# Two factors taken out of the build order's reckoning in a Mamba and mixture-of-experts layer

## The chip, the cores and the metric

The kernel runs on one core of one Trainium2 chip. The metric is the device time of one execution in microseconds (us). Engines: PE is TensorE (matmuls and transposes; its weight loads are listed apart as PEld), DVE is VectorE, ACT is ScalarE, POOL is GpSimd, SP is SyncE, which here only issues DMAs.

## The reference

One layer on x of 4 sequences x 1024 steps x 512 channels, all float32. Cut to what matters:

```python
sa, ca, ga, sb, cb, gb = modulation(silu(c) @ wmod)      # per sequence, 6 x 512
h = layernorm(x) * (1 + ca) + sa
u = causal_depthwise_conv(h, conv_w, 4 taps) + conv_b
dt, Bm, Cm = split(u @ xproj_w.T, [128, 16, 16])
delta = softplus(dt @ dtproj_w.T + dtproj_b)
# scan over time, 16 states for each of 512 channels
h_t = exp(delta * A) * h_(t-1) + delta * u * Bm ;  y_t = sum_n h_t[n] * Cm[n]
x = x + ga * (y + u * D_skip)
h = layernorm(x) * (1 + cb) + sb
logits = tanh(h @ Wg1.T) @ Wg2.T                         # 8 experts, the top 2 chosen
down[e] = silu(h @ Wup[e].T + bup[e]) @ Wdown[e].T + bdown[e]     # 512 -> 256 -> 512
x = x + gb * sum_e scores[e] * down[e]
```

## The kernel before

**Blocks and stages.** Time is cut into blocks of 512 steps: two for each of the first three sequences, and 512, 384 and 128 for the last, eight blocks in all. `front(blk)` makes the layernorm, convolution and projections of a block. The recurrence takes a block as 128 units, one for each of 16 states and 4 chunks of 128 channels. For a unit the steps are:

- `products_b` (L892 on ACT, or L899 on POOL): dB, the product of delta * u with a column of B, with time on partitions, in buffers of two units;
- `inputs` (L935, PE): up to four transposes of dB into the PSUM tile pb, of which there are two;
- `decays` (L920, ACT): exp(delta * A) into the tile h, four buffers of two units;
- `recurrences` (L950, DVE): the scan along time, from h and pb, in place in h;
- `products_c` (L967, POOL): hc = h * C, C's row having come by a broadcast load cq (L868, issued on SP, four buffers); then a copy of the last state (L975);
- `sums` (L1006, PE): transposes of hc that accumulate over the 16 states in PSUM.

`back(blk)` then makes the second layernorm and the router and scatters each token's row, for its two experts, to a DRAM buffer sorted by expert (L1335, an indirect DMA of POOL). `tiles(g)` and `expert` take 128 sorted rows at a time, 86 tiles in all: a load of the rows and of the expert's weights (1,025 KB, issued on SP, four buffers `w`), transposes (L1407), the first product (L1420), bias, tanh and gate (L1431, L1438, L1440), the second product (L1448), the scaling (L1458) and a store. `combine` fetches the rows back by indirect DMAs that add (L1497). The last block of 128 tokens goes instead through all eight experts (`dense`, L1550 to L1615).

**The order.** Nothing is scheduled on the chip: each engine runs its instructions in the order in which the builder wrote them. The builder writes them by a reckoning of its own, the class `Order`. Each piece of work above is a generator, a thread, that yields one step at a time: an engine (or a choice of engines), a cost, and what it depends on. `run` finds the step that could start first, looks at the steps on the same engine that could start within `TOGETHER` (0.15 us) after that, and takes the one whose thread has the earliest due time. It moves the engine's clock on by the cost, says when the result may be used (`HANDOFF`: 0.30 us after PE, 0.17 after DVE, 0.22 after ACT, 0.12 after POOL), and lets the generator go on, which writes the instructions. Buffers are handed out in the same reckoned time, so the order sets which buffer a tile gets too. Threads with a due time below `URGENT` (the last two blocks') get a window of 0.8 us (`AHEAD`).

The costs are formulas in the number n of elements per partition: a matmul `t_mm` 2 x 0.00084 n us (a float32 product is two instructions), a transpose `t_tr` 0.11, ACT `t_act` 0.19 + 0.00083 n, DVE `t_dve` 0.09 + 0.00104 n, a scan `t_scan` 0.09 + 0.00215 n, POOL `t_pool` 0.05 + 0.0024 n. Where a step leaves the engine open (`either`, `both`, `products_b`), `begins` chooses by these bare costs. A transfer is reckoned at 290 KB/us shared, 150 KB/us alone, and 4.0 us besides (L107). Due times go by 150 us for a block of 512 steps (`DUE`, L265).

Between the formula and the engine's clock stand two factors (L101, L102, used at L234 and L235): every cost over 0.03 us is multiplied by `PACE`, which is 1.1 for PE and 1.0 for the others, and `WAIT` is added, 0.06 us on DVE, ACT and POOL.

Of the kernel before, what the change touches and what calls it, by code (L numbers as in the profile page):

```python
# [97 lines left out]

PE, DVE, ACT, POOL, SP = range(5)
HANDOFF = (0.30, 0.17, 0.22, 0.12, 0.0)  # L100
PACE = (1.1, 1.0, 1.0, 1.0, 1.0)  # L101
WAIT = (0.0, 0.06, 0.06, 0.06, 0.0)  # L102
TOGETHER = 0.15
URGENT = -1e3
AHEAD = 0.8
# [78 lines left out]
class Order:  # L184
# [34 lines left out]
    def run(self):  # L219
        while self.threads:  # L220
            can = [(b, th) for th in self.threads if (b := self.begins(th)) is not None]
            if not can:
                raise RuntimeError("no thread can go on: " + str([th[0].__name__ for th in self.threads]))
            t0, eng, _ = min(can, key=lambda c: c[0][0])[0]
            (t, _, cost), th = min(
                (
                    c
                    for c in can
                    if c[0][1] == eng and c[0][0] <= t0 + (AHEAD if c[1][3] < URGENT else TOGETHER)
                ),  # L230
                key=lambda c: c[1][3],
            )
            self.eng, kb = eng, th[1][4]
            if cost > 0.03:  # L234
                cost = cost * PACE[eng] + WAIT[eng]  # L235
            self.start = t
            self.free[eng] = t + cost
            self.fin = t + cost + HANDOFF[eng]
            if kb:
                self.moved[eng] = max(self.moved[eng], t + cost) + kb / KB_PER_US  # L240
                self.fin = max(self.moved[eng], t + cost + kb / KB_ALONE) + TRANSFER
            th[2] = self.fin
            th[3] += th[4]
            self.advance(th)
# [1486 lines left out]
```

## Time and profile before

| | before |
|---|---|
| three runs | 1471.55, 1481.65, 1467.81 us; median 1471.55 |
| profiled execution | 1473.26 us; its span from first to last instruction 1471.5 us |
| mean granted TensorE clock | 0.925 of full speed |
| busy: PE, DVE, ACT, POOL | 1236.6, 1146.8, 1041.7, 1052.8 us |
| weight loads (PEld) | 931.7 us |
| DMA | 321.65 MB, mean 219 GB/s |
| first scan starts, last scan starts | 67.7 us, 1387.6 us |

Busy time is the time in which an engine executes; waits, semaphore instructions and the issuing of DMAs are not counted. The ends of matmuls are modelled, so PE's busy time is no measure of how near it is to its peak. The granted clock is the share of TensorE's full speed that the chip allowed in a stretch. A wait is shown as "engine, tile, line <- what ended it".

### The profile page before, as it was taken

The numbers are of one execution on the slowest core, as the hardware profiler recorded it, in microseconds if no ns is written. First come the engines' busy times: TensorE is split into PE (matmuls) and PEld (weight loads), VectorE is DVE, ScalarE is ACT, GpSimd is POOL, SyncE is SP. The second block draws the span as 40 slices with busy tenths as digits, with TensorE's granted clock in tenths as the row PEclk, the third lists the DMA queues.
The fourth block names the chain that finished last, engine by engine and source line by source line (L and its number), as shares of the span: only waits on it lengthen the run. The fifth ranks groups of instructions, "written<-read, shape, count | busy, mean of one in ns | idle before, by whom it ended". The sixth has DMA issues, their size and how long they took to land. (4 is left out here: it accounts for less than half of the span.)

```text
span 1471.5 us, 24433 instructions
## 1 busy us (share of the span) xinstructions
PE 1236.6 (84%) x7716; PEld 931.7 (63%) x7716; DVE 1146.8 (78%) x1860; ACT 1041.7 (71%) x2086; POOL 1052.8 (72%) x1239
## 2 busy tenths in 40 slices
PE   5588777878788988988888888998798898888886
PEld 1447564656477766775667766786587776764653
DVE  3569999889887898998887888897879879556343
ACT  3679898689687684899676776888678877455210
POOL 1368897898687676888888656798788878656222
PEclk8699899889799998999699999999999999998798
DMA  4367664758688997654679968688999986986997
GB/s 175 101 161 157 136 160 101 197 127 199 140 243 283 292 273 202 213 159 101 197 257 313 309 210 204 219 269 246 262 252 271 281 221 219 337 249 200 298 311 200
DMA packets 141935, 321.65 MB, mean 219 GB/s; under 512 B 14899, under 2 KB 43475, under 8 KB 128998
## 3 DMA queue, kind: packets, MB, share of 16 engines
q1 hardware_dynamic: 111344, 254.35, 57.9%
q0 software_dynamic: 13888, 32.58, 9.9%
q10 hardware_dynamic: 16566, 33.08, 8.8%
q8 instruction: 63, 1.03, 0.3%
q14 instruction: 74, 0.61, 0.1%
HBM read 245.95 MB, written 82.40 MB: 223 GB/s over the span
## 5 line engine op out<-in xcount | busy, mean ns | idle before, releaser
L967 POOL TENSOR_TENSOR hc<-h,cq 128x512 f32<-128x512 f32 (+2 forms) x576 | 689.5, 1255 | 190.1 <-PE acc L1006 53.4
L920 ACT ACTIVATE h<-delta,a_neg 128x512 f32<-128x512 f32 (+2 forms) x576 | 370.8, 667 | 88.8 <-POOL state L975 44.9
L892 ACT ACTIVATE dB<-duT,bT 128x256 f32<-128x256 f32 x801 | 359.9, 499 | 77.2 <-PE pb L935 74.8
L935 PE MATMUL pb<-ident,dB 128*128 128x128 f32 x2048 | 344.6, 291 | 80.4 <-DVE h L950 64.3
L1006 PE MATMUL acc<-ident,hc 128*128 128x128 f32 x2048 | 340.9, 291 | 75.1 <-POOL hc L967 73.2
L950 DVE TENSOR_TENSOR_SCAN h<-h,state,pb 128x512 f32<-128x512 f32 (+2 forms) x320 | 330.6, 1054 | 50.9 <-PE pb L935 25.8
L935 PEld LDWEIGHTS pb<-ident,dB 128*128 128x128 f32 x2048 | 251.2, 149 | 169.3 <-DVE h L950 85.9
L1006 PEld LDWEIGHTS acc<-ident,hc 128*128 128x128 f32 x2048 | 250.5, 148 | 155.9 <-POOL hc L967 122.3
L950 DVE TENSOR_TENSOR_SCAN h<-h,pb 128x512 f32<-128x512 f32 x256 | 304.4, 1207 | 45.9 <-PE pb L935 37.2
L1420 PE MATMUL pe<-xT,w 128*128 128x128 f32 x1376 | 188.0, 282 | 6.5 <-ACT xT L351 4.8
L1420 PEld LDWEIGHTS pe<-xT,w 128*128 128x128 f32 x1376 | 174.1, 197 | 27.4 <-issue 14.2
L1448 PE MATMUL po<-w,hid 128*128 128x512 f32 x344 | 180.8, 612 | 6.6 <-DVE hid L1440 6.5
L899 POOL TENSOR_TENSOR dB<-duT,bT 128x512 f32<-128x512 f32 (+1 forms) x115 | 119.6, 1061 | 18.4 <-PE pb L935 12.4
L1497 POOL DMA_INDIRECT xc<-xs,idx x56 | 90.4, 1614 | 51.7 <-DMA xc<-xs,idx 29.8
L1458 DVE SCALAR_TENSOR_TENSOR xs<-po,xs,gbh 128x512 f32<-128x512 f32 x86 | 63.6, 740 | 39.7 <-PE po L1448 38.1
L1335 POOL DMA_INDIRECT xs<-h,idx x62 | 64.0, 1032 | 41.3 <-POOL idx L1334 9.2
L1448 PEld LDWEIGHTS po<-w,hid 128*128 128x128 f32 x344 | 54.1, 195 | 24.0 <-issue 11.3
L1438 ACT ACTIVATE th<-pe 128x256 f32<-128x256 f32 x86 | 32.2, 377 | 49.4 <-DVE pe L1431 49.2
L351 ACT COPY xT<-px 128x512 f32<-128x512 f32 x79 | 45.5, 577 | 25.0 <-PE px L1407 24.5
L975 POOL COPY state<-h 128x2 f32<-128x2 f32 x160 | 54.6, 341 | 0.1
L720 PE MATMUL pxd<-xpg,u 128*128 128x160 f32 x256 | 46.2, 329 | 9.4 <-issue 5.6
L1407 PE MATMUL px<-ident,xs 128*128 128x128 f32 x344 | 53.8, 284 | 0.3 <-DVE u L688 0.3
(196 smaller groups left out, 1533.5 us busy)
## 6 DMA issues: line engine op xcount, KB each, us to landing
w<-w_all SPq DMA_DIRECT2D x86, 1025.0 KB, 8.5
cq<-scr SPq DMA_DIRECT2D x224, 256.0 KB, 5.3
xs<-xs SPq DMA_DIRECT2D x86, 256.5 KB, 5.3
xs<-xs SPq DMA_DIRECT2D x86, 256.0 KB, 8.0
xs<-xc ACTq DMA_DIRECT2D x16, 1026.0 KB, 11.7
we<-w_all SPq DMA_DIRECT2D x8, 1025.0 KB, 12.3
xf<-in_x SPq DMA_DIRECT2D x32, 256.0 KB, 6.9
xr<-in_x SPq DMA_DIRECT2D x14, 512.0 KB, 8.9
```

The lines of the kernel that those rows point to most:

```text
L892: nc.scalar.activation(dB[u // 2].t[:, t, :], duT_sb[blk][half].t[:, t, :], AF.Identity, scale=bT_sb[blk].t[:, t, n : n + 1],)
L899: engine().tensor_tensor(dB[u // 2].t[:, t0:t1, :], duT_sb[blk][half].t[:, t0:t1, :], bT_sb[blk].t[:, t0:t1, n].unsqueeze(2).to_broadcast( ...
L920: nc.scalar.activation(hs[u // 2].t[:, i, :ln], delta_sb[blk][half].t[:, i, :ln], AF.Exp, scale=a_neg[:, dc, n : n + 1])
L935: nc.tensor.transpose(pbs[u][:, t * P : (t + 1) * P], dB[u // 2].t[:, t, i * P : (i + 1) * P], ident)
L950: nc.vector.tensor_tensor_scan(h, h, pbs.pop(u)[:, :ln], 0.0 if t0 == 0 else state[:, n, dc : dc + 1], ALU.mult, ALU.add,)
L967: nc.gpsimd.tensor_tensor(hcs[u].t[:, :ln], hs[u // 2].t[:, i, :ln], cq[u // 2].t[:, :ln], ALU.mult)
L1006: nc.tensor.matmul(acc[blk, dc][:, t * P : (t + 1) * P], lhsT=src.t[:, t * P : (t + 1) * P], rhs=ident, is_transpose=True, start=False, st ...
L1335: i = nc.gpsimd.indirect_dma_start(out=xs_d[g], out_offset=bass.IndirectOffsetOnAxis(ap=idx[:, k, t : t + 1], axis=0), in_=h2[k].t, in_off ...
L1420: nc.tensor.matmul(pu[:, hc * P : (hc + 1) * P], lhsT=up[:, kc, hc * P : (hc + 1) * P], rhs=xT.t[:, kc, :], start=(kc == 0), stop=(kc == D ...
L1448: nc.tensor.matmul(po, lhsT=hid.t[:, hc * P : (hc + 1) * P], rhs=w.t[:, W_DN + hc * D : W_DN + (hc + 1) * D], start=(hc == 0), stop=(hc == ...
L1458: nc.vector.scalar_tensor_tensor(xs.t[:, :D], po, xs.t[:, D:], gbh[b].t, ALU.mult, ALU.mult)
L1497: nc.gpsimd.indirect_dma_start(out=a, out_offset=None, in_=xs_d[g], in_offset=bass.IndirectOffsetOnAxis(ap=idx_sb[blk][:, choice, t : t + ...
```

## The change

The two factors go out of the reckoning. Costs are taken as the formulas give them, on every engine; the handoffs, the transfer times, the due times and the windows stay, and so do the buffers and the due times of the last blocks. No line that writes an instruction is touched.

```diff
@@ -98,8 +98,6 @@
 
 PE, DVE, ACT, POOL, SP = range(5)
 HANDOFF = (0.30, 0.17, 0.22, 0.12, 0.0)
-PACE = (1.1, 1.0, 1.0, 1.0, 1.0)
-WAIT = (0.0, 0.06, 0.06, 0.06, 0.0)
 TOGETHER = 0.15
 URGENT = -1e3
 AHEAD = 0.8
@@ -231,8 +229,6 @@
                 key=lambda c: c[1][3],
             )
             self.eng, kb = eng, th[1][4]
-            if cost > 0.03:
-                cost = cost * PACE[eng] + WAIT[eng]
             self.start = t
             self.free[eng] = t + cost
             self.fin = t + cost + HANDOFF[eng]
```

## The prediction

> **What bounds the kernel now.** I read the page's busy shares first, then the waits, then the clock by stretches, then single rows. The page:
>
> ```profile
> span 1471.5 us, 24433 instructions
> PE 1236.6 (84%) x7716; PEld 931.7 (63%) x7716; DVE 1146.8 (78%) x1860; ACT 1041.7 (71%) x2086; POOL 1052.8 (72%) x1239
> ```
>
> No engine is full, and four stand within 13 points of each other. So the time is set by how the four streams interlock, and that is what the build order decides: each engine takes its instructions strictly in the order in which the builder wrote them, and an instruction put too early holds up all behind it. The waits, by engine and releaser (us in all, times, longest):
>
> ```profile
> PE acc L1006 <- POOL hc L967: 73.2, 101, 6.0
> PE pb L935 <- DVE h L950: 64.3, 65, 3.9
> DVE h L950 <- PE pb L935: 63.0, 66, 5.7
> DVE xs L1458 <- PE po L1448: 38.1, 32, 5.2
> DVE pe L1431 <- PE pe L1420: 17.9, 13, 3.3
> POOL hc L967 <- DMA cq<-scr: 12.9, 7, 7.3
> ```
>
> DVE waits on PE for 63.0 + 38.1 + 17.9 = 119.0 us, out of 1471.5 - 1146.8 = 324.7 us in which it is idle: 37%. PE in turn stands at the head of its queue for POOL and DVE, 73.2 + 64.3 = 137.5 us. Waits in both directions mean that neither is the bound; the order is wrong now one way and now the other.
>
> **The clock.** Stretches of the trace (us from the start; columns PE, weight loads, DVE, ACT and POOL busy with counts, granted clock, DMA share, GB/s):
>
> ```profile
> 375.00:400.00 25.00, 19.11 (x68) 12.33 (x69) 22.08 (x51) 15.38 (x30) 17.22 (x26) 0.61 0.50 122
> 400.00:700.00 300.00, 263.66 (x1778) 209.54 (x1777) 258.47 (x396) 234.66 (x452) 233.77 (x251) 0.96 0.76 221
> 700.00:725.00 25.00, 21.04 (x79) 13.12 (x78) 21.22 (x39) 15.39 (x32) 19.60 (x30) 0.64 0.66 186
> ```
>
> The mean granted clock is 0.925, and the loss is lumped: 0.61 and 0.64 where PE had 68 and 79 instructions in 25 us, 0.96 where it had 1778 in 300 us (148 per 25). What it does to a step is in the timeline (start, length, engine, line), together with two ACT rows that I use below:
>
> ```profile
> 700.90 0.72 ACT L920 ACTIVATE h<-delta,a_neg 128x512 f32<-128x512 f32 x1
> 701.53 0.89 ACT L892 ACTIVATE dB<-duT,bT 128x256 f32<-128x256 f32 x2
> ...
> 707.04 0.66 PE L1006 MATMUL acc<-ident,hc 128*128 128x128 f32 x4 [0.81 <-POOL hc L967]
> ...
> 712.33 1.11 PE L1006 MATMUL acc<-ident,hc 128*128 128x128 f32 x4
> ```
>
> The same four transposes take 0.66 us, and 5 us later 1.11 us.
>
> **Are the removed pads true?** The builder reckons a step at its formula, times 1.1 on PE, plus 0.06 us on DVE, ACT and POOL. Rows, shapes kept apart (busy us, mean ns of one):
>
> ```profile
> L967 POOL TENSOR_TENSOR hc<-h,cq 128x512 f32<-128x512 f32 x448 | 590.3, 1366 | 134.6 <-DVE h L950 48.7 <-PE acc L1006 20.1 <-DMA cq<-scr 11.9
> L920 ACT ACTIVATE h<-delta,a_neg 128x512 f32<-128x512 f32 x448 | 311.3, 714 | 53.3 <-POOL state L975 30.5 <-POOL hc L967 19.6 <-DVE mv_a L594 3.0
> L950 DVE TENSOR_TENSOR_SCAN h<-h,state,pb 128x512 f32<-128x512 f32 x192 | 239.7, 1267 | 16.1 <-PE pb L935 14.7 <-ACT dB L892 0.4
> L1448 PE MATMUL po<-w,hid 128*128 128x512 f32 x344 | 180.8, 612 | 6.6 <-DVE hid L1440 6.5
> ```
>
> By length of a row the pads are right: hc 1.366 us against a formula of 1.279 (padded 1.339), the scan 1.267 against 1.191 (1.251), the decay 0.714 against 0.615 (0.675). By spacing they are not: the decay at 700.90 is followed at 701.53 by the next instruction, 0.63 us later, because one instruction's end overlaps the next one's start; that is the bare formula. On PE, 172 products of the second expert matrix (two instructions each) are 180.8/172 = 1.05 us of busy time each, against 0.86 bare and 0.946 padded. So the PE factor is the pad that the chip confirms (1/0.925 = 1.08), and the 0.06 is partly a stand-in for what the formula leaves out.
>
> The Trainium skill's "TensorE: Matmul & The Clock Gate" (Part 1: the HAM clock gate) says that the clock is halved by default and released by sustained activity. The stretches above agree in direction (0.61 at 68 instructions, 0.96 at 148). Taken alone the rule would make the full clock the right reckoning wherever PE is dense, and the PE term below would be 0 there; the trace's mean of 0.925 decides for me.
>
> **The change part by part.** It adds no instruction and no wait to the program, and takes none away: 0 us of work. Only the order on each queue changes, with the buffers that follow from it, DMA issues included.
>
> (1) The common part cancels. In the builder's count of its steps, 1,641 on DVE, 1,373 on ACT and 1,077 on POOL carry 0.06 us: 98, 82 and 65 us. PE's bare sum is about 1,054 us (the largest terms: 4,096 transposes of dB and hc at 0.11 = 451; 688 products of the first expert matrix at 0.224 = 154; 172 of the second at 0.86 = 148), so its pad is 105 us. A reckoning in which all engines are faster by one factor gives the same order. The pair that paces the recurrence shrinks by 0.06/1.251 = 4.8% (scan) and 0.06/1.339 = 4.5% (hc); the PE steps by 0.1/1.1 = 9.1%. What is left is 9.1 - 4.6 = 4.5% of 1,054 = 47 us of PE work that the order now believes it can fit in beside the recurrence. Against DVE as a whole, short steps included (98 of some 1,193 us reckoned, 8.2%), it would be only 0.9%, 9 us.
>
> (2) What a misplaced microsecond of PE costs. The order changes by what fits in ahead of the next transposes of dB (L935): an expert matmul (0.86 us) or a projection goes first. On the chip, PE then reaches L935 late; queued behind are the products of C's sums (L1006), and the scan (L950) waits, then hc (L967) and the decay's buffer. No row shows this change, so bounds from both sides: every one of the 47 us puts off a scan, +47; every one fills a wait that PE has now (137.5 us are there to be filled), and makes the work after it earlier, -47. I take the share of DVE's idle time that PE causes, 37%: 47 x 0.37 = +17 us. In the other 63% DVE has other work or another reason to wait, and the delay is covered; if that cover is gone it is the +47.
>
> (3) Handoffs (0.12 to 0.30 us) and transfer times (4.0 us and 290 KB/us) stay, so they look some 5% longer against the work. An expert's load of 1,284 KB is reckoned at 1284/150 + 4.0 = 12.6 us while the row for it shows 8.5 us to landing, so 5% of 12.6 = 0.6 us later for each of 86 tiles. It hides behind four weight buffers; uncovered it is 0.6 x 86 = 52 us. I take 0. On the SP queue the 288 loads of C's rows (L868) trade places with tile loads and stores; DMA cq delays hc by only 12.9 us today. I take 0 here and price the bad case as a rival.
>
> (4) The choice of ACT or POOL for dB compares bare costs in both versions; only the times at which engines come free move. If 10 of the 115 POOL products (1.06 us) go to ACT (0.80 us), that is -11 and +8 us on engines that are idle 419 and 430 us. Taken as 0, bounds -10 to +10.
>
> (5) Start (before the first scan) and tail (after 1388 us: the last block's experts, one load after another) have little to choose from: 0.
>
> **The sum.** The profiled execution took 1473.3 us (span 1471.5 and 1.8 around it), 1.7 us above the median of the runs. 1473.3 + 17 = 1490; against the median that is 1489 us.
>
> **Rivals.** A: *no net effect.* The 4.5% is below what an order feels; as many steps gain as lose. For it: waits in both directions of about the same size (119.0 and 137.5 us). Against it: the two are not equally harmful, since DVE is nearer to full than POOL. It gives the median again, 1472 us.
>
> B: *faster.* The place is PE's wait at L1006 for hc. Without the pads the order holds back less: PE takes an expert's product in the 73.2 us where it now stands for POOL, and tiles finish earlier, so that fewer DVE instructions meet the recurrence. For it: the 0.63 us spacing, by which the bare costs of ACT are the true ones. Price: half of the larger bound, -23 us, 1449 us. It decides as soon as PE's early work is done in such waits more often than ahead of L935: from one half on the sign turns.
>
> C: *a queue is caught.* With compute reckoned faster, loads of C's rows stand behind a tile load on SP that waits for a weight buffer; POOL's hc starves. Today that happens 7 times, longest 7.3 us. If one load in eight of the 288 comes 1.8 us late (12.9/7), it is 36 x 1.8 = 65 us: 1538 us. Against it: C's loads carry due times 20 us ahead and have four buffers.
>
> D: *the edit doesn't bite.* Only if every choice stayed the same; 4,000 steps lose a pad and choices are made within 0.15 us, so I give it no chance of its own; it would look like A.
>
> **How the numbers follow.** Forecast (own range 1477 to 1505) 0.48, A 0.28, B 0.14, C 0.10. The range 1456 to 1521 leaves out most of B and most of C, under 2 in 10, and takes in +47 (1519). About 1% (15 us) is what a measurement of this kernel can tell from no change; the runs of before span 13.9 us. Above 1486: C, three quarters of the forecast and a little of A, 0.49. Below 1457: B and a trifle, 0.14. Between: 0.37.
>
> **What would show it.** Same counts on PE and DVE; ACT and POOL differ only by moved dB products. Right: DVE's waits on PE (L935, L1448, L1420) rise from 119 us towards 136, and the scans' last start moves from 1388 us to about 1404. Step 1 is wrong if PE's wait for hc and h falls well below 137.5 us while DVE's does not rise; step 3 if the SP queue's waits before L868 delay hc by far more than 12.9 us. The forecast is wrong if the time falls below 1477, or if the granted clock moves by more than 0.02: then the order has changed the clock, which I hold at 0.925.

## The result and the profile after

The changed kernel takes 1472.5 us (median of 20 runs, 1457.7 to 1485.2) against 1472.2 us for the kernel before (20 runs, 1465.5 to 1481.7): a ratio of 1.000 with a 95% interval of 0.998 to 1.002. The change makes no difference that can be measured. The forecast was 1489 us; what happened is rival A. The profiled execution of the changed kernel took 1475.7 us, 1474.0 of it span. Its page begins (span, then busy time of each engine, share and count):

```profile
span 1474.0 us, 24473 instructions
PE 1241.7 (84%) x7716; PEld 941.4 (64%) x7716; DVE 1152.3 (78%) x1857; ACT 1053.0 (71%) x2116; POOL 1039.8 (71%) x1228
```

PE's count is the same. ACT has 30 instructions more and POOL 11 fewer, mostly because 12 of the 115 products dB moved from POOL to ACT. Lines of the changed kernel stand four lower than before, so L946 is the scan that was L950. The waits of the changed kernel, in the order in which those of before were shown (us, times, longest):

```profile
PE acc L1002 <- POOL hc L963: 66.6, 81, 5.1
PE pb L931 <- DVE h L946: 67.1, 81, 4.1
DVE h L946 <- PE pb L931: 64.3, 72, 3.3
DVE xs L1454 <- PE po L1444: 58.1, 41, 5.0
DVE pe L1427 <- PE pe L1416: 28.5, 19, 5.0
POOL hc L963 <- DMA cq<-scr: 11.3, 7, 4.1
```

The order did change, and in the forecast direction: DVE now waits 64.3 + 58.1 + 28.5 = 150.9 us for PE, against 119.0. But DVE's whole idle time is 1474.0 - 1152.3 = 321.7 us, against 324.7. These three lines are not all: added up over every line of the two lists, DVE's waits for PE rose from 168.9 to 197.4 us, and its waits for ACT fell from 110.6 to 91.6. What it waits for has another name; how long it waits is the same. The scan's row (count, shortest/median/longest in ns, first and last start in us) shows the pace:

```profile
L946 DVE TENSOR_TENSOR_SCAN h<-h,state,pb x320: 450/1253/1281, 191.3 to 1395.3; 128x512 f32<-128x512 f32 x96, 128x384 f32<-128x384 f32 x32, 128x128 f32<-128x128 f32 x32
```

The last scan starts at 1395.3 us, against 1387.6, in one execution of each; the first starts at 64.6 us, against 67.7. The clock did not move much: 0.918 against 0.925 on the mean, and the same places are slow (columns as in the prediction):

```profile
375.00:400.00 25.00, 18.54 (x67) 12.55 (x66) 21.35 (x50) 15.82 (x30) 16.80 (x25) 0.60 0.47 106
400.00:700.00 300.00, 263.18 (x1779) 209.70 (x1777) 258.37 (x399) 238.05 (x461) 229.30 (x249) 0.96 0.79 222
700.00:725.00 25.00, 19.25 (x84) 12.89 (x83) 22.92 (x41) 16.17 (x34) 20.81 (x28) 0.72 0.76 208
```

### The profile page after: what moved, and what is told of

Same layout as the page of the kernel before. It is cut to its first block, busy times and chain, and to the rows that moved or that the text cites. A ratio compares the mean times of both kernels' runs of the same rounds, so it can differ in the third digit from the quotient of the medians.

```text
span 1474.0 us, 24473 instructions
## 1 busy us (share of the span) xinstructions
PE 1241.7 (84%) x7716; PEld 941.4 (64%) x7716; DVE 1152.3 (78%) x1857; ACT 1053.0 (71%) x2116; POOL 1039.8 (71%) x1228
## 4 chain that ended last, share of the span: by engine, by line
PE 45%; DVE 23%; POOL 9%; DMA 8%; issue 7%; ACT 6%; ACTq 0%; POOLq 0%; SPq 0%; DVEq 0%
DVE h L946 10%; PE pb L931 8%; PE acc L1002 8%; PE po L1444 7%; PE pe L1416 7%; POOL hc L963 6%; PE pxd L716 2%; DMA cq<-scr 2%; DMA xs<-xs 2%; PE pc L1193 2%; PE pl L1083 2%; ACT dB L888 2%; DVE pu L684 2%; ACT h L916 1%; DMA xc<-xs,idx 1%
## 5 line engine op out<-in xcount | busy, mean ns | idle before, releaser
L888 ACT ACTIVATE dB<-duT,bT 128x256 f32<-128x256 f32 x829 | 372.4, 499 | 72.8 <-PE pb L931 67.1
L931 PE MATMUL pb<-ident,dB 128*128 128x128 f32 x2048 | 350.2, 295 | 82.0 <-DVE h L946 67.1
L1002 PE MATMUL acc<-ident,hc 128*128 128x128 f32 x2048 | 341.6, 291 | 68.3 <-POOL hc L963 66.6
L946 DVE TENSOR_TENSOR_SCAN h<-h,state,pb 128x512 f32<-128x512 f32 (+2 forms) x320 | 330.0, 1053 | 50.1 <-PE pb L931 32.1
L931 PEld LDWEIGHTS pb<-ident,dB 128*128 128x128 f32 x2048 | 256.7, 151 | 167.4 <-DVE h L946 85.1
L946 DVE TENSOR_TENSOR_SCAN h<-h,pb 128x512 f32<-128x512 f32 x256 | 304.5, 1208 | 45.7 <-PE pb L931 32.2
L1444 PE MATMUL po<-w,hid 128*128 128x512 f32 x344 | 184.8, 626 | 13.3 <-DVE hid L1436 12.9
L895 POOL TENSOR_TENSOR dB<-duT,bT 128x512 f32<-128x512 f32 (+1 forms) x103 | 105.6, 1040 | 33.3 <-PE pb L931 21.7
L1454 DVE SCALAR_TENSOR_TENSOR xs<-po,xs,gbh 128x512 f32<-128x512 f32 x86 | 63.8, 742 | 58.3 <-PE po L1444 58.1
L1427 DVE TENSOR_TENSOR pe<-pe,w 128x256 f32<-128x256 f32 x86 | 36.2, 421 | 32.2 <-PE pe L1416 28.5
```

The source lines that it names most:

```text
L888: nc.scalar.activation(dB[u // 2].t[:, t, :], duT_sb[blk][half].t[:, t, :], AF.Identity, scale=bT_sb[blk].t[:, t, n : n + 1],)
L895: engine().tensor_tensor(dB[u // 2].t[:, t0:t1, :], duT_sb[blk][half].t[:, t0:t1, :], bT_sb[blk].t[:, t0:t1, n].unsqueeze(2).to_broadcast( ...
L931: nc.tensor.transpose(pbs[u][:, t * P : (t + 1) * P], dB[u // 2].t[:, t, i * P : (i + 1) * P], ident)
L946: nc.vector.tensor_tensor_scan(h, h, pbs.pop(u)[:, :ln], 0.0 if t0 == 0 else state[:, n, dc : dc + 1], ALU.mult, ALU.add,)
L1002: nc.tensor.matmul(acc[blk, dc][:, t * P : (t + 1) * P], lhsT=src.t[:, t * P : (t + 1) * P], rhs=ident, is_transpose=True, start=False, st ...
L1444: nc.tensor.matmul(po, lhsT=hid.t[:, hc * P : (hc + 1) * P], rhs=w.t[:, W_DN + hc * D : W_DN + (hc + 1) * D], start=(hc == 0), stop=(hc == ...
```

## The experiments

Each ratio below is against the kernel before, timed on the same chip in the same set of runs (the kernel before takes 1469 to 1490 us, depending on the chip); microseconds are ratio less one, times that median. In brackets, 95% intervals. The theories: **1**, the prediction's, that a microsecond of PE which the reckoning doesn't know of costs 0.37 us; **2**, that orders of about this accuracy are all worth the same; **3**, that the two halves of the change have opposite effects that cancel.

### Halves of the change, and random orders

Edits against the kernel before, `pads_only` and `factor_only`:

```diff
-PACE = (1.1, 1.0, 1.0, 1.0, 1.0)
+PACE = (1.0, 1.0, 1.0, 1.0, 1.0)
```

> The reckoning with 0.06 us on DVE, ACT and POOL steps, and PE at its bare formula: half of the change. Theory 1 (the prediction's step 2: PE reckoned too fast against the scan puts PE work ahead of the scan's transposes, at 37% of its size): the relative shift is now 9.1% of 1,054 us of PE work, 96 us, so 0.37 x 96 = +35 us, about 1507 us. Theory 2 (the order is a draw: any order that this builder makes within some per cent of the costs lands within about 10 us of 1472): 1462 to 1482. Theory 3 (the two parts have opposite effects that cancel in the change): clearly off 1472 here, and off the other way with the other half.

```diff
-WAIT = (0.0, 0.06, 0.06, 0.06, 0.0)
+WAIT = (0.0, 0.0, 0.0, 0.0, 0.0)
```

> The reckoning with the factor 1.1 on PE and without the 0.06 us: the other half of the change. Theory 1: PE is now reckoned 4.6% slower against the scan than before, the shift goes the other way, 0.37 x 48 = -18 us, about 1454 us. Theory 2 (a draw): 1462 to 1482. Theory 3 (opposite effects cancel): off 1472 by as much as the run with the pads only, the other way.

Edit against the changed kernel, `jitter_1` (seed 1), `jitter_3` (seed 3) and, with 0.5 in place of 0.08, `jitter_wide` (seed 2):

```diff
+            cost *= 1.0 + 0.08 * (self.rnd.random() - 0.5)
             self.start = t
             self.free[eng] = t + cost
```

> The changed kernel, with every cost of the reckoning multiplied by a random number from 0.96 to 1.04 (seed 1): another order of the same kind, with no bias of one engine against another. Theory 1 (a bias between the engines' costs is what counts): 1472 within 5 us. Theory 2 (a draw): within 10 us of 1472, and different from it by more than the interval. If it is off by 20 us or more, the order matters far more than the change showed, and the change's zero is a coincidence.

> The changed kernel with random factors from 0.96 to 1.04 on all costs, seed 3: one more draw beside the changed kernel (ratio 1.000), pads only (1.002), factor only (1.000) and seed 1 (0.996). Theory 2 (a draw): within 0.5% of before. Theory 1: 1.000 within 0.3%.

> The changed kernel, with every cost of the reckoning multiplied by a random number from 0.75 to 1.25 (seed 2): errors about three times as large as the pads that went out (5 to 9%), without a bias between the engines. Theory 2 (a draw: errors of some per cent make another order of the same quality): within 1% of before even here, since errors of single steps average out over a unit. A rival (the order is good only as far as the reckoning is true, and its quality falls with the size of the error): 2 to 4% slower.

| run | what is reckoned | ratio to before |
|---|---|---|
| the change | bare costs | 1.000 [0.998, 1.002] |
| pads_only | 0.06 us on DVE, ACT, POOL | 1.0021 [0.9992, 1.0050] |
| factor_only | 1.1 on PE | 1.0004 [0.9979, 1.0030] |
| jitter_1 | bare, within 4% | 0.9963 [0.9938, 0.9989] |
| jitter_3 | bare, within 4% | 1.0028 [0.9987, 1.0069] |
| jitter_wide | bare, within 25% | 1.0106 [1.0062, 1.0150] |

Theory 1 put the halves at +35 and -18 us; they measured +3 and +1. Theory 3 falls too: neither half does anything that can be measured alone. Random errors of up to 4% give orders within 0.4% of before. Even errors of up to 25% on every step cost only 1.1%, in the one draw made: just over the 1% of theory 2 and less than the 2 to 4% of the rival there. Because seed 1 was the first order that looked better, it ran again:

> The order of jitter_1 once more, with more rounds: it was 0.4% faster than before (interval 0.1 to 0.6%). If this belongs to the order, 0.3 to 0.5% faster again; if it was a chance of that set of runs, within 0.2% of before.

It measured 0.9985 [0.9955, 1.0014]: most of the 0.4% was chance, and no order here is shown to be better than the one before.

### How wrong the reckoning must be

`pe_0_6`, `pe_0_8` and `pe_1_6` reckon PE at 0.6, 0.8 and 1.6 of its formula, `all_1_2` every engine at 1.2; all without the 0.06 us. The first as a diff against the kernel before:

```diff
-PACE = (1.1, 1.0, 1.0, 1.0, 1.0)
-WAIT = (0.0, 0.06, 0.06, 0.06, 0.0)
+PACE = (0.6, 1.0, 1.0, 1.0, 1.0)
+WAIT = (0.0, 0.0, 0.0, 0.0, 0.0)
```

> PE reckoned at 0.6 of its formula, the others bare: about 420 us of PE work that the order does not know of, nine times the shift of the prediction's step 1. Theory 1 (37% of it reaches the end): +155 us, about 11% slower. Theory 2 (taken up by waits): under 3% slower; if it is within 1%, the reckoning of PE hardly matters at all.

> PE reckoned at 0.8 of its formula, the others bare: 211 us of PE work that the order does not know of. At 0.6 (422 us) the time was 4.3% above before, 62 us, so 0.15 us for each us. Linear price: 0.15 x 211 = 31 us, 2.1% slower. Flat bottom (small errors are free, the price sets in beyond some 10 to 20%): at most 1% slower. Theory 1 with its 37%: 78 us, 5.3%.

> PE reckoned at 1.6 of its formula: the reckoning makes PE the bound (1,054 x 1.6 = 1,690 us), so DVE, ACT and POOL steps are placed late and loosely. Theory 1 (PE held back is harmless to the scan): not slower than before. Theory 2: slower by 1 to 5%, because the order is now made for another machine, in which PE's due times alone decide. It tells on which side a wrong factor costs.

> Every engine's bare cost times 1.2, handoffs and transfers as they are: a common factor, over twice what the pads were. The prediction's step 1 says that a common factor cancels: within 1% of before. If it is slower by over 1%, the handoffs and transfer times against the costs matter, which the prediction took as 0 in step 3.

| PE reckoned at | 0.6 | 0.8 | 1.0 (the change) | 1.1 (factor_only) | 1.6 | all at 1.2 |
|---|---|---|---|---|---|---|
| ratio to before | 1.0428 [1.0371, 1.0485] | 1.0041 [1.0005, 1.0077] | 1.000 | 1.0004 | 1.1273 [1.1222, 1.1324] | 1.0113 [1.0043, 1.0183] |

The bottom is flat. At 0.8, where 211 us of PE work are unknown to the order, the loss is 6 us; at 0.6 (422 us) it is 63 us. A price in proportion, from the run at 0.6, would have been 31 us at 0.8. On the other side, 1.6 costs 187 us, three times as much as 0.6. Both runs lie outside every range that I had given them (3% and 11% for 0.6, at most 5% for 1.6). The common factor of 1.2 was expected to cancel within 1% and did not quite: +1.1%. Handoffs and transfers looked shorter by a sixth there, and the window of 0.15 us and the due times stayed too; which of these it was I did not separate. The mean granted clock was lower as well, 0.909 against 0.924 for the kernel before in the same set.

The run at 0.6 also shows why the waits misled me. The same three of DVE's waits for PE:

```profile
DVE xs L1458 <- PE po L1448: 57.1, 55, 3.1
DVE h L950 <- PE pb L935: 46.8, 59, 3.3
DVE pe L1431 <- PE pe L1420: 46.5, 34, 5.9
```

Together 150.4 us, the same as the changed kernel's 150.9, while the one is 4.3% slower and the other not at all. The full lists do tell the two apart: all of DVE's waits for PE come to 168.9 us before, 197.4 in the changed kernel and 228.2 here. But the first 28 us of that rise cost nothing.

### The price of a microsecond, by engine

In these the order is the changed kernel's, and work is added behind the reckoning's back: `pe_more` transposes the last part of dB twice for each of 576 units, `pe_more4` all of it. (There are nine blocks of 64 units, one for each state and chunk, not the eight of 128 that the description of the kernel gives.)

```diff
 for t in range(nt):
     nc.tensor.transpose(pbs[u][:, t * P : (t + 1) * P], dB[u // 2].t[:, t, i * P : (i + 1) * P], ident)
+    if t == nt - 1:      # pe_more4: without this condition
+        nc.tensor.transpose(pbs[u][:, t * P : (t + 1) * P], dB[u // 2].t[:, t, i * P : (i + 1) * P], ident)
```

> The changed kernel's order, with one transpose of dB more for each of 576 units (the last of the unit done twice, same result): 576 x 0.107 us = 62 us of PE work at full clock that the reckoning does not know of. Theory 1 (37% of an unreckoned microsecond of PE reaches the end): +23 us, 1495. Theory 2 (PE work that the order does not reckon with is taken up by PE's waits for POOL and DVE, 134 us in the changed kernel): less than +8 us. If it is +50 or more, PE is the bound.

> The changed kernel's order, with all transposes of dB done twice: 2,048 x 0.107 = 219 us of PE work at full clock that the order does not know of, against 62 us in the run with one more per unit (+5 us against before). If PE's waits take it up until they are gone (134 us for hc and h, 232 us idle in all): a kink, under 0.1 us for each us up to some 130 us and about 1 beyond, so +60 to +100 us. If linear at 0.08: +18 us. Theory 1 with 37%: +81 us, but then the first 62 us should have cost 23.

`act_more` and `pool_more` add a small copy after each decay and each product hc, `dve_more` after each scan:

```diff
+    spare = const.tile([P, 16], F32, name="spare")
...
+            nc.scalar.copy(spare[:, :1], ident[:, :1])              # act_more
+            nc.gpsimd.tensor_copy(spare[:, :16], ident[:, :16])     # pool_more
+            nc.vector.tensor_copy(spare[:, :16], ident[:, :16])     # dve_more
```

> The changed kernel's order, with a copy of one column on ACT after each of the 576 decays, unreckoned: by the intercept of the ACT formula 0.19 us each, 109 us of ACT time. ACT is idle for 421 us. If ACT's idle time is slack: under +15 us. If waits are shared out so that any engine's time counts at 37%: +40 us.

> The changed kernel's order, with a small copy (128x16) on POOL after each of the 576 products hc, unreckoned: by the spacing of the small state copies (0.14 us) 81 us of POOL time. POOL is idle for 434 us. If slack: under +12 us. If POOL paces the recurrence (PE's sums wait for hc 66.6 us, and ACT's decays wait for the buffers that hc frees): +40 us or more.

> The changed kernel's order, with a small copy (128x16) on DVE after each of the 576 scans, unreckoned. By the spacing of such small copies (60 to 100 ns) it is 35 to 58 us of DVE time. If DVE's stream is what sets the time (it is the fullest of the three elementwise engines, and its idle time is waits inside that stream), nearly all of it arrives: +30 to +55 us. If DVE's idle time is slack, as PE's is (62 us more gave 5 us against before), under +10 us.

`dve_more` came out 6.1% slower [5.6, 6.5], 90 us, and its copies were not what I had costed. Their row (shortest, median, longest in ns), and one of them in the timeline beside POOL (start, length):

```profile
L955 DVE COPY spare<-ident x576: 135/150/7274, 65.1 to 1490.5; 128x16 f32<-128x16 f32 x192
```

```profile
404.69 2.50 POOL L965 TENSOR_TENSOR hc<-h,cq 128x512 f32<-128x512 f32 x2
405.14 1.20 DVE L947 TENSOR_TENSOR_SCAN h<-h,pb 128x512 f32<-128x512 f32 x1
406.27 2.31 DVE L955 COPY spare<-ident 128x16 f32<-128x16 f32 x1
407.13 0.18 POOL L973 COPY state<-h 128x2 f32<-128x2 f32 x1
407.27 1.27 POOL L965 TENSOR_TENSOR hc<-h,cq 128x512 f32<-128x512 f32 x1
408.50 0.74 DVE L1201 TENSOR_TENSOR xr<-xr,pc 128x256 f32<-128x256 f32 x2
```

The copy ends at 408.58, 0.04 us after POOL's product (408.54). So two runs took the copy from pb in PSUM instead, 16 columns into the spare tile (`dve_psum`) or 128 columns in place (`dve_psum128`):

```diff
-                pbs.pop(u)[:, :ln],
+                pbs[u][:, :ln],
...
+            nc.vector.tensor_copy(spare, pbs.pop(u)[:, :16])          # dve_psum
+            p = pbs.pop(u)                                            # dve_psum128
+            nc.vector.tensor_copy(p[:, :128], p[:, :128])
```

> The changed kernel's order, with a small copy (128x16) on DVE after each scan, this time from pb in PSUM: 576 x about 0.08 us = 46 us of DVE time. In the run with the copy from SBUF 152 of the 576 copies took over 0.3 us, 164 us together, and nearly all of these ended about 30 ns after the POOL instruction under way. If that was a wait for POOL, it is gone here: no copy over 0.3 us, and the time +10 to +45 us over before (by DVE's own price of 0.2 to 1 per us). If the 90 us came from DVE being full, the price per us here is about 2 and the time +90 us.

> As the run before, with 128 columns copied in place in pb: by the formula 576 x 0.22 = 127 us of DVE time, three times as much. If DVE sets the time: +100 us or more. If a microsecond on DVE counts in part as on the others (PE 0.08 to 0.1, POOL about 0.1): +15 to +60 us, and rising faster than in proportion as DVE's idle time of 322 us is used up.

```profile
L955 DVE COPY spare<-pb x576: 135/148/151, 66.2 to 1403.6; 128x16 f32<-128x16 f32 x192
```

No copy from PSUM is longer than 0.151 us. All of these runs together; for PE the added work is 576 or 2,048 times 0.107 us, an estimate (in the changed kernel's trace most transposes of dB follow each other at 0.109 us), for the others the rise of busy time over the changed kernel's profile:

| run | added | ratio to before | us | price per us |
|---|---|---|---|---|
| pe_more | PE 62 us | 1.0034 [1.0000, 1.0067] | 5 | 0.08 |
| pe_more4 | PE 219 us | 1.0375 [1.0321, 1.0430] | 56 | 0.26; beyond the first 62: 0.32 |
| dve_psum | DVE 37 us | 1.0025 [0.9987, 1.0062] | 4 | 0.10 |
| dve_psum128 | DVE 148 us | 1.0496 [1.0443, 1.0550] | 74 | 0.50; beyond the first 37: 0.63 |
| pool_more | POOL 78 us | 1.0070 [1.0043, 1.0098] | 10 | 0.13 |
| act_more | ACT 47 us | 0.9948 [0.9911, 0.9985] | -8 | below 0 |

I had expected one of the engines to show itself as the one that sets the time. None does: the first 37 to 78 us on PE, DVE or POOL cost about a tenth of their length, and only larger additions, tried on PE and DVE, cost a third to two thirds of what is beyond that. `dve_psum` lies below the +10 to +45 us I gave it, `dve_psum128` between its two ranges (+15 to +60, and +100 or more).

Some of these prices are not of the added work alone. PE's clock rose with the work: the mean granted clock is 0.934 in `pe_more` and 0.961 in `pe_more4`, against 0.917 and 0.918 for the kernel before in the same sets. The stretch from 375 to 400 us, where the changed kernel had 0.60 with 67 instructions, in `pe_more` and in `pe_more4`:

```profile
375.00:400.00 25.00, 17.62 (x86) 12.39 (x85) 22.93 (x53) 19.62 (x38) 17.62 (x27) 0.73 0.45 100
375.00:400.00 25.00, 20.87 (x164) 17.43 (x162) 20.70 (x43) 22.63 (x43) 17.62 (x24) 1.00 0.51 111
```

So part of the added work is offset by the rest of PE's work running faster (the 2,048 transposes of the sums are busy for 322.2 us in `pe_more4` and 341.6 in the changed kernel): PE's busy time rose by 38.8 us for the 62 added and by 152.7 for the 219. Per microsecond of that rise the prices are 0.13 and 0.37, though PE's busy time is modelled. And in `dve_psum128` the copy, 0.30 us long on the mean, also keeps pb from PE:

```profile
PE pb L931 <- DVE pb L955: 143.9, 189, 5.1
```

That is 143.9 us against 67.1 for the scan's release of pb in the changed kernel, a rise as large as the whole loss of 74 us. DVE's own time and the later pb are not separated.

PE's waits show where its work went. The two largest, in `pe_more` and then in `pe_more4`:

```profile
PE pb L931 <- DVE h L950: 63.1, 77, 3.7
PE acc L1006 <- POOL hc L967: 57.2, 66, 5.6
```

```profile
PE pb L931 <- DVE h L949: 42.0, 52, 3.2
PE acc L1005 <- POOL hc L966: 25.6, 41, 4.7
```

That is 63.1 + 57.2 = 120.3 and 67.6 us, against 133.7 in the changed kernel. `pe_more4` used up 66 us of these waits; the kink that I expected at 130 us, with full price after it, is softer than that. And DVE's wait for pb, 72.0 us in `pe_more`, rises far only in `pe_more4`:

```profile
DVE h L949 <- PE pb L934: 112.7, 143, 3.1
```

112.7 us against 64.3. `act_more` was faster than before although it adds work, so it ran again:

> The run with 576 copies more on ACT once more: it was 0.5% faster than before, although it adds work. If ACT's idle time is slack and the rest was chance: within 0.3% of before. If again 0.5% faster, the added copies shift when something else starts, and that is worth 0.5%.

The second set gave 0.9974 [0.9945, 1.0002]. ACT's 47 us cost nothing that can be measured; that they help is not shown.

## Why the prediction was wrong

**No work added or removed, and the choice of ACT or POOL (4): right.** PE's count is unchanged, DVE's differs by three, and 12 products dB moved where I reckoned with 10. **Queues and loads (3): right.** POOL's wait for C's rows is 11.3 us against 12.9. **The clock held (0.918 against 0.925), and start and tail (5) are nearly as before:** the first scan starts 3 us earlier, and from the start of the last one it is 79 us to the end against 84.

**The common part cancels (1): not shown either way.** Neither the pads alone nor the factor alone moves the time, so there was nothing to see cancel, and no run measures how much PE work really moved, the 47 us. The 1.2 on all engines costs 1.1%, so at 20% something does not cancel. One reading in it is wrong: in the builder's count 1,373 steps are DVE's (82 us) and 1,641 ACT's (98 us). Against DVE as a whole the shift is then 9.1 - 6.9 = 2.2%, 23 us instead of 9; the forecast used neither. And what the prediction saw on ACT, that by spacing the pads are not true, the trace shows on all three engines: from a 128x512 row to the next on its engine it is 0.61 us for the decay, 1.23 for hc and 1.17 for the scan (medians in the kernel before), none of them above its bare formula. The change made the reckoning truer there and, by the mean clock of 0.925, less true on PE; neither half is felt.

**The price of misplaced PE work (2): this is the step that failed.** I took 37% of 47 us, +17 us, from the share of DVE's idle time that PE ends. Measured, PE work that the order does not know of costs 0.08 us per us up to 62 us (`pe_more`); 0.08 x 47 is 4 us, about what the interval of the result (3 us either way) can hide. A wrong factor is cheaper still, and with the clock as it was (0.919 against 0.917): at 0.8 it costs 6 us for 211 us, 0.03 per us, or 1.4 us for 47. The error has two parts. A wait is ended by whichever input comes last, so its name says nothing of what the wait would have been had that input come earlier. The three waits rose by 32 us, more than the 17 I looked for; the sign that I had named for being right came true, while other waits shrank by as much and the time did not move. (That DVE's idle time did not rise is no second proof: with the same work on DVE, idle time moves only as the time does.) The 37% is not even the share it was called: all of DVE's waits for PE are 168.9 of 324.7 us, 52%, and would have given +24. And I used a share, as if every microsecond cost the same; a price of 0.3 exists, but only for lateness well beyond this change's. A likely reason is that the buffers (two pb, four dB, four h, three hc) let an engine come late for a while without holding up the next, but no run changes their number, so this is not shown.

**The rivals.** A was right, in its result and in its first sentence, that the shift is below what an order feels: 20% on PE and random errors of 4% are hardly felt either. Its other argument, waits of similar size in both directions, was nearer to the cause than mine: PE's 133.7 us of waits for POOL and DVE are where PE's extra work can go, and in `pe_more4` half of them are gone. B did not happen: PE's wait at the sums fell only from 73.2 to 66.6 us. C did not happen.

What stays open: why PE reckoned 60% too slow costs three times what PE reckoned 40% too fast does, and what shares the time out among four engines of which none is full. The runs show that a small addition is far from full price on each of the four (on DVE with the copy from PSUM), and that larger ones, tried on PE and DVE alone, cost more per microsecond.

## What to carry to other kernels

A build order made from reckoned costs sits on a flat bottom: errors of 5 to 9% in the costs changed nothing here, random ones of up to 25% cost 1%, a bias of 20% on one engine 0.4%, and only biases of 40 and 60% were dear. Before pricing a change of order from a list of waits, add known work to the engine in question, once a little and once three times as much: the first gives the price that counts for a small change, the second shows where the slack ends. Read the clock along with it, since work added on PE raised it here. A wait that grows on one line is no loss if the engine's other waits shrink by as much, so add up all of an engine's waits, not the few longest.

## What the runs showed of the hardware

A copy of 16 elements per partition on DVE, from SBUF to SBUF, takes 0.15 us, but 152 of 576 took over 0.3 us, 164 us together, and 147 of these ended 28 to 43 ns after the end of a product on POOL. The same copy from PSUM never took more than 0.151 us. The Trainium skill's "SBUF — State Buffer" (SBUF: two separate sides) says that DVE, in a mode that uses two ports, and POOL share one pair of ports as an exclusive lock, and that the later one is blocked for the other's whole instruction. The rows agree that the copy is blocked. It can also be blocked for longer than one instruction: the copy in the timeline above waited through the end of one product and the whole of the next, which began after it, and 29 of the 152 waited through one to five such products. In this kernel 37 us of such copies from PSUM cost 4 us, and the same number from SBUF cost 90. POOL's waits for the copy itself do not make the difference: they are 69.6 us with PSUM and 90.0 with SBUF.
